# Two graph layers on one Trainium2 core: scores in seven block products instead of eight, and another order of the stages

## The chip, the cores and the metric

The kernel runs on one core of a Trainium2 chip. The metric is the time of one execution on the device, in microseconds (us). Three runs of the kernel before gave 1820.88, 1821.27 and 1821.62 us; the median is 1821.27. One further execution was recorded by the profiler; every duration in this document comes from such a record.

## The reference, cut to what matters

The input x holds 64 items of 256 tokens with 512 features. `adj` is a 256 x 256 matrix of zeros and ones. Two layers follow each other:

```
h   = relu(layernorm(x))
q, k, v = h Wq^T, h Wk^T, h Wv^T
rel = adj^T * (q k^T)                  # elementwise mask, per item 256 x 256
rel = rel / norm(rel, axis=2)
x   = x + rel v
h   = relu(layernorm(x))
x   = x + (adj h) weight + bias
```

Everything is in f32.

## The kernel before, in words

**Tiling.** Two items make a pair of 512 tokens; there are NP = 32 pairs, and the loop in `pairs` (line 431) turns once per pair. Wq and Wk are folded into one matrix M once at the start, so that scores are h M h^T. The stages of a pair are:

- `ln0` (L224): layer norm and ReLU of x into h. `norm` (L186) is statistics on VectorE (L196, L197), a square root on ScalarE (L199) and a few small operations.
- h^T: `place_blocks` (L245) moves the 32 x 32 blocks of h to their transposed places by 16 DMAs on the SP queue, into the tile hp; `transpose_blocks` (L256) then transposes inside each block on VectorE (L260), eight instructions.
- `project_g` (L266), G = M^T h^T, and `project_v` (L279), v = h Wv^T.
- `scores` (L292): h G, 16 matmuls of 256 moving columns; mask on VectorE (L304), squares on ScalarE (L305), a sum of squares on GpSimd (L307).
- `attend` (L310): the product with v (L317, banks pu), the norms (L326, pn: a column of ones times the sums of squares), and x + rel v (L331).
- `norm` again and `ln1_relu` (L337): the ReLU result h2c is split into an fp32r part (cast on ScalarE, L220) and the rest (subtraction on VectorE, L221), together h2s; h2c has two buffers, each for one of the four 128-token chunks. GpSimd adds the bias to x (L346).
- `gather` (L348): adjacency times h2s (L360, banks py), 32 fp32r matmuls, copied to yt by ScalarE (L364).
- `mix` (L372): the last product, with `weight`, added to x (L377); then the transfer out (L381) on the queue of GpSimd.

**The seven block products.** G, V and the last product are done by the scheme of `winograd` (L140), Strassen's algorithm in Winograd's form: each matrix is cut in 2 x 2 blocks, sums of blocks are made first (`left_sums` L127, `right_operands` L111), and seven block products take the place of eight. The products go into three PSUM banks, a, b and c. Banks a and c are not cleared between products: a product adds to what the bank holds, and `take` reads the bank after each. So a product into a bank waits for the reader of the product before in that bank:

```python
        product(bank_a, 6, False)
        take(0, 1, bank_a, True)
        product(bank_c, 3, False)
        take(0, 1, bank_c, False)
        product(bank_a, 7, False)
        take(1, 1, bank_a, False)
        product(bank_b, 2, True)
        take(0, 0, bank_b, False)
        product(bank_a, 4, False)
        take(1, 0, bank_a, True)
```

The first time a block of the result is taken it is copied by ScalarE, the second time it is added by VectorE (in `mix`, always added by VectorE). Scores alone are done by eight block products' worth of plain matmuls.

**What sets the order.** Each engine works through its own instructions in order. A scheduler that runs when the kernel is built puts the instructions of each engine in an order, starting from that of the program and by its own estimates of when each operand is ready; it inserts the waits. PSUM has seven banks for products (`ps_m`), taken in turn, and one for pn. Tiles of the pool `work` have one buffer each: h^T (`ht`), its sums (`hs`), G, v, rel, h2s, yt. The loads of x rotate through four tiles of `xpool`, after a first tile of its own.

In the loop before, turn i puts on TensorE: scores(i), last product(i-1), product with v and pn(i), G(i+1), V(i+1), adjacency(i).

Of the kernel before, what the change touches and what calls it, by code (L numbers as in the profile page):

```python
# [9 lines left out]
F32 = mybir.dt.float32  # L10
# [8 lines left out]
def kernel(  # L19
# [33 lines left out]
    nc = tc.nc  # L53
# [16 lines left out]
    const = ctx.enter_context(tc.tile_pool(name="const", bufs=1))  # L70
    xpool = ctx.enter_context(tc.tile_pool(name="xpool", bufs=4))
    work = ctx.enter_context(tc.tile_pool(name="work", bufs=1))
# [4 lines left out]

    X, H, HP, HT, HS, G, V, R, H2, Y, YS = ({} for _ in range(11))

    def load(i):  # L80
        pool, tag = (const, "x_first") if i == 0 else (xpool, "x")
        X[i] = pool.tile([P, NB, NC, D], F32, tag=tag, name=f"x_{i}")
        nc.sync.dma_start(out=X[i], in_=xs[i])
# [26 lines left out]

    def right_operands(w, name):  # L111

        def blk(j, k):
            return w[:, j * HC : (j + 1) * HC, k * HD : (k + 1) * HD]

        t = [const.tile([P, HC, HD], F32, name=f"{name}_t{n}") for n in range(1, 5)]
        nc.vector.tensor_sub(t[0], blk(0, 1), blk(0, 0))
        nc.vector.tensor_sub(t[1], blk(1, 1), t[0])
        nc.vector.tensor_sub(t[2], blk(1, 1), blk(0, 1))
        nc.vector.tensor_sub(t[3], blk(1, 0), t[1])  # L120
        return {1: blk(0, 0), 2: blk(1, 0), 3: blk(1, 1), 4: t[3], 5: t[0], 6: t[1], 7: t[2]}

# [3 lines left out]

    def left_sums(at, tag, i):  # L127
        s = work.tile([P, 4, HC, HT_], F32, tag=tag, name=f"{tag}_{i}")
        a = left_blocks(at)
        nc.vector.tensor_add(s[:, 0], a(1, 0), a(1, 1))  # L130
        nc.vector.tensor_sub(s[:, 1], s[:, 0], a(0, 0))
        nc.vector.tensor_sub(s[:, 2], a(0, 0), a(1, 0))
        nc.vector.tensor_sub(s[:, 3], a(0, 1), s[:, 1])
        return s

    def left_operands(at, s):
        a = left_blocks(at)
        return {1: a(0, 0), 2: a(0, 1), 3: s[:, 3], 4: a(1, 1), 5: s[:, 0], 6: s[:, 1], 7: s[:, 2]}

# [33 lines left out]
    def product_weights_moving(left, right):  # L173
# [9 lines left out]
        return product  # L183


    def norm(src):  # L186

        st = small.tile([P, TC, 6], F32, tag="st", name="st")
        mv = small.tile([P, TC, 2], F32, tag="mv", name="mv")
        rs = small.tile([P, TC], F32, tag="rs", name="rs")
        nb = small.tile([P, TC], F32, tag="nb", name="nb")
        for c in range(TC):
            nc.vector.bn_stats(st[:, c, :], src[:, c, :])  # L196
            nc.vector.bn_aggr(mv[:, c, :], st[:, c, :])  # L197
        nc.vector.tensor_scalar(rs, mv[:, :, 1], 0.0, EPS, op0=ALU.max, op1=ALU.add)
        nc.scalar.activation(rs, rs, AF.Sqrt)  # L199
        nc.vector.reciprocal(rs, rs)  # L200
        nc.vector.scalar_tensor_tensor(nb, mv[:, :, 0], -1.0, rs, op0=ALU.mult, op1=ALU.mult)  # L201
        return rs, nb

    def relu_chunk(dst, src, scale_shift, c):
        rs, nb = scale_shift
        nc.scalar.activation(  # L206
            dst, src[:, c, :], AF.Relu, bias=nb[:, c : c + 1], scale=rs[:, c : c + 1]
        )
# [13 lines left out]


    def ln0(i):  # L224
        pool, tag = (const, "h_first") if i == 0 else (work, "h")
        H[i] = pool.tile([P, TC, D], F32, tag=tag, name=f"h_{i}")
        relu(H[i], flat(X[i]), norm(flat(X[i])))

    def new_ht(i):
        HT[i] = work.tile([P, DC, NC, NB * P], F32, tag="ht", name=f"ht_{i}")  # L230
        return HT[i]

    def transposes_by_matmul(i):
        h, ht = H.pop(i), new_ht(i)
        for d in range(DC):
            pt = ps_m.tile([P, T], F32, tag="pm", name="pt")
            for half in range(NC):
                for b in range(NB):
                    nc.tensor.transpose(
                        pt[:, ts(half * NB + b, P)], h[:, b * NC + half, ts(d, P)], ident  # L240
                    )
            nc.scalar.copy(ht[:, d].rearrange("p h t -> p (h t)"), pt)
        HS[i] = left_sums(ht, "hs", i)

    def place_blocks(i):  # L245

        h = H.pop(i)
        HP[i] = work.tile([P, TC, DC, P], F32, tag="hp", name=f"hp_{i}")
        hv = h.rearrange("p c (d e) -> p c d e", e=P)
        for j in range(P // S):  # L250
            for k in range(P // S):
                nc.sync.dma_start(
                    out=HP[i][ts(j, S), :, :, ts(k, S)], in_=hv[ts(k, S), :, :, ts(j, S)]
                )

    def transpose_blocks(i):  # L256
        hp, ht = HP.pop(i), new_ht(i)
        for d in range(DC):
            for half in range(NC):
                nc.vector.transpose(  # L260
                    ht[:, d, half].rearrange("p (b n) -> p b n", b=NB),
                    hp.rearrange("p (b h) d n -> p b h d n", b=NB)[:, :, half, d],
                )
        HS[i] = left_sums(ht, "hs", i)

    def project_g(i):  # L266
# [9 lines left out]

        winograd(product_tokens_moving(left_operands(HT[i], HS[i]), m_right), take)

    def project_v(i):  # L279
# [9 lines left out]

        winograd(product_weights_moving(left_operands(HT[i], HS[i]), wv_right), take)  # L290

    def scores(i):  # L292
        ht, g = HT.pop(i), G.pop(i).rearrange("p e h (b n) -> p e h b n", b=NB)
        rel = work.tile([P, NB, NC, N], F32, tag="rel", name=f"rel_{i}")
        sq = work.tile([P, NB, NC, N], F32, tag="sq", name=f"sq_{i}")
        for b in range(NB):
            pm = ps_m.tile([P, NC, N], F32, tag="pm", name="prel")
            for m in range(NC):
                for e in range(DC):
                    nc.tensor.matmul(  # L300
                        pm[:, m, :], ht[:, e, m, ts(b, P)], g[:, e, :, b, :],
                        start=(e == 0), stop=(e == DC - 1),
                    )
            nc.vector.tensor_mul(rel[:, b], pm, adj_sb)  # L304
            nc.scalar.activation(sq[:, b], rel[:, b], AF.Square)  # L305
        sqs = work.tile([P, NB, N], F32, tag="sqs", name=f"sqs_{i}")
        nc.gpsimd.tensor_tensor(sqs, sq[:, :, 0], sq[:, :, 1], ALU.add)  # L307
        R[i] = (rel, sqs)

    def attend(i):  # L310
        (rel, sqs), v, xt = R.pop(i), flat(V.pop(i)), flat(X[i])
        pu = []
        for b in range(NB):
            for n in range(NC):
# [6 lines left out]
                pu.append(pm)  # L321
        pn = ps_n.tile([P, TC], F32, tag="pn", name="pn")
        for b in range(NB):
            for n in range(NC):
                c = b * NC + n
                nc.tensor.matmul(pn[:, c : c + 1], sqs[:, b, ts(n, P)], ones, start=True, stop=True)  # L326
        rn = small.tile([P, TC], F32, tag="rn", name="rn")
        nc.scalar.activation(rn, pn, AF.Sqrt)  # L328
        nc.vector.reciprocal(rn, rn)
        for c in range(TC):  # L330
# [38 lines left out]
    def gather_sums(i):  # L369
        YS[i] = left_sums(Y[i], "ys", i)  # L370

    def mix(i):  # L372
# [5 lines left out]

        winograd(product_weights_moving(left_operands(Y.pop(i), YS.pop(i)), w_right), take)
        if i + 1 < NP:  # L380
# [44 lines left out]
    ln0(0)  # L425
    m_right = right_operands(m_sb, "m")
    wv_right = right_operands(wvt_sb, "wv")
    w_right = right_operands(w_sb, "w")


    def pairs(exact):
        for j in (1, 2):
            if j < NP:
                load(j)
        transposes_by_matmul(0)
        if NP > 1:
            ln0(1)
            place_blocks(1)
        project_v(0)
        project_g(0)  # L440
        for i in range(NP):
            nxt = i + 1 < NP
            if i + 3 < NP:
                load(i + 3)
            scores(i)
            if i > 0:
                gather_sums(i - 1)
            if i > 0 and nxt:
                mix(i - 1)
            if nxt:  # L450
                transpose_blocks(i + 1)
            attend(i)
            if nxt:
                project_g(i + 1)
            scale_shift = norm(flat(X[i]))
            if nxt:
                project_v(i + 1)
            elif i > 0:
                mix(i - 1)
            ln1_relu(i, scale_shift, exact)  # L460
            if i + 2 < NP:
                ln0(i + 2)
                place_blocks(i + 2)
            gather(i, exact)
        gather_sums(NP - 1)
        mix(NP - 1)

# [34 lines left out]
```

## Time and profile before

| | |
|---|---|
| median of 3 runs | 1821.27 us |
| profiled execution: its own time / span of its instructions | 1820.87 / 1819.1 us |
| PE (TensorE matmul) busy | 1790.7 us, 98% |
| DVE (VectorE) busy | 1003.3 us, 55% |
| ACT (ScalarE) busy | 534.4 us, 29% |
| POOL (GpSimd) busy | 254.5 us, 14% |
| granted TensorE clock | 0.999 of full speed |
| HBM traffic | 39 GB/s over the span |

How to read it: the span runs from the first to the last instruction of the program; the 1.8 us between it and the execution's own time lie around it. "PEld" is TensorE's weight load, which overlaps its matmuls. An f32 matmul is recorded as two passes, each with a weight load; a pass starts when the one before has streamed its columns, so the distance between starts, not the duration of one record, is its cost. In a row of instructions the arrow points from what is read to what is written ("out<-in"), then come shapes, count, busy time and mean duration, and after the bar the idle time of that engine just before and what ended it. In a timeline row the first two numbers are start and length in us. Engines that are not the bottleneck may idle without cost.

### The profile page before, as it was taken

How to read it: one execution, taken by the hardware profiler on the slowest of the kernel's cores; microseconds unless marked ns; L12 is line 12 of the kernel's file. 1: busy time of each engine (PE TensorE's matmuls, PEld its weight loads, DVE VectorE, ACT ScalarE, POOL GpSimd, SP SyncE). 2: the span in 40 equal slices, each digit the busy share in tenths (PEclk: the TensorE clock that was granted, in tenths of full speed). 3: DMA queues.
4: the chain of work that ended last, by engine and by line, in shares of the span. 5: the costliest groups of instructions: out<-in, count | busy, mean ns of one | idle time of the engine just before them, and what ended most of it. 6: DMA issues, size and time to landing. Idle time of an engine off the chain costs nothing.

```text
span 1819.1 us, 21280 instructions
## 1 busy us (share of the span) xinstructions
PE 1790.7 (98%) x8262; PEld 1470.8 (81%) x8262; DVE 1003.3 (55%) x1992; ACT 534.4 (29%) x943; POOL 254.5 (14%) x200
## 2 busy tenths in 40 slices
PE   7999999999999999999999999999999999999998
PEld 4788887888888888878888878888788888788886
DVE  4555566545556545665455565456654555654554
ACT  3223332223332133322233321333222333213321
POOL 0101111111111011111011110111110111101111
PEclk9999999999999999999999999999999999999999
DMA  6122221221221222212212212222122122122101
GB/s 223 21 47 47 47 70 49 68 70 24 70 60 57 70 47 47 70 50 68 70 24 70 61 56 70 47 47 70 50 66 70 24 70 62 55 70 47 24 24 49
DMA packets 290239, 105.83 MB, mean 58 GB/s; under 512 B 263120, under 2 KB 263120, under 8 KB 290128
## 3 DMA queue, kind: packets, MB, share of 16 engines
q1 hardware_dynamic: 279904, 68.19, 17.9%
q0 software_dynamic: 8592, 33.03, 4.8%
q10 hardware_dynamic: 1632, 3.15, 0.5%
q8 instruction: 67, 1.10, 0.2%
q14 instruction: 44, 0.36, 0.1%
HBM read 38.27 MB, written 33.55 MB: 39 GB/s over the span
## 4 chain that ended last, share of the span: by engine, by line
PE 66%; DVE 23%; ACT 9%; DMA 1%; issue 1%; DVEq 0%; ACTq 0%
PE bank_a L178 19%; PE prel L300 12%; PE pu L317 12%; DVE st L196 8%; PE py L360 7%; PE bank_c L178 7%; DVE h2s L221 7%; PE bank_b L178 6%; DVE x L331 4%; ACT h2c L206 4%; DVE g L275 2%; ACT h2s L220 2%; ACT v L286 2%; ACT h L206 1%; PE pn L326 1%; PE bank_a L166 1%
## 5 line engine op out<-in xcount | busy, mean ns | idle before, releaser
L346 POOL TENSOR_TENSOR x<-x,bias_bc 128x512 f32<-128x512 f32 x128 | 187.9, 1494 | 526.2 <-ACT h2c L206 512.8
L300 PE MATMUL prel<-g,ht 128*128 128x256 f32 x1024 | 226.4, 379 | 0.7 <-ACT g L273 0.7
L317 PE MATMUL pu<-v,rel 128*128 128x512 f32 x512 | 224.9, 592 | 0.0
L300 PEld LDWEIGHTS prel<-g,ht 128*128 128x128 f32 x1024 | 192.3, 190 | 26.0 <-ACT g L273 1.1
L317 PEld LDWEIGHTS pu<-v,rel 128*128 128x128 f32 x512 | 97.3, 190 | 108.8 <-issue 107.1
L221 DVE TENSOR_TENSOR h2s<-h2c,h2s 128x512 fp32r<-128x512 f32 x128 | 128.4, 1041 | 83.6 <-ACT h2s L220 83.6
L328 ACT ACTIVATE rn<-pn 128x4 f32<-128x4 f32 x32 | 5.5, 173 | 564.1 <-PE pn L326 564.1
L196 DVE BATCH_NORM_STATS2 st<-x 128x6 f32<-128x512 f32 x256 | 167.1, 665 | 7.2 <-DMA x<-in_x_dram 7.2
L377 DVE TENSOR_TENSOR x<-bank_a,x 128x512 f32<-128x512 f32 x128 | 88.4, 691 | 108.1 <-PE bank_a L178 108.1
L307 POOL TENSOR_TENSOR sqs<-sq 128x512 f32<-128x512 f32 x32 | 40.6, 1268 | 699.0 <-issue 594.5
L360 PE MATMUL py<-adjt_r,h2s 128*128 128x256 f32 x1024 | 134.8, 289 | 0.1
L178 PE MATMUL bank_a<-wv_t,hs 128*128 128x256 f32 x512 | 127.0, 391 | 7.4 <-ACT v L286 5.1
L360 PEld LDWEIGHTS py<-adjt_r,h2s 128*128 128x128 f32 x1024 | 127.3, 191 | 2.5 <-DVE h2s L221 0.8
L178 PEld LDWEIGHTS bank_a<-wv_t,hs 128*128 128x128 f32 x512 | 92.5, 190 | 40.9 <-ACT v L286 30.7
L206 ACT ACTIVATE h2c<-x,nb,rs 128x512 f32<-128x512 f32 x128 | 100.7, 810 | 80.8 <-DVE mv L197 53.1
L178 PE MATMUL bank_a<-w_t,ys 128*128 128x256 f32 x512 | 121.1, 379 | 1.2 <-DVE x L377 1.2
L166 PE MATMUL bank_a<-hs,m_t 128*128 128x256 f32 x512 | 121.0, 379 | 0.0
L178 PEld LDWEIGHTS bank_a<-w_t,ys 128*128 128x128 f32 x512 | 97.2, 190 | 14.7 <-DVE x L377 1.6
L166 PEld LDWEIGHTS bank_a<-hs,m_t 128*128 128x128 f32 x512 | 97.3, 190 | 13.2
L304 DVE TENSOR_TENSOR rel<-prel,adj_sb 128x512 f32<-128x512 f32 x64 | 44.2, 691 | 115.3 <-PE prel L300 115.3
L206 ACT ACTIVATE h<-x,nb,rs 128x512 f32<-128x512 f32 x128 | 96.8, 807 | 30.3 <-DVE nb L201 30.3
L305 ACT ACTIVATE sq<-rel 128x512 f32<-128x512 f32 x64 | 40.3, 629 | 206.4 <-DVE rel L304 206.4
(104 smaller groups left out, 2712.4 us busy)
## 6 DMA issues: line engine op xcount, KB each, us to landing
x<-in_x_dram SPq DMA_DIRECT2D x32, 1024.0 KB, 5.5
hp<-h SPq DMA_DIRECT2D x496, 64.0 KB, 2.3
out_dram<-x POOLq DMA_DIRECT2D x31, 1024.0 KB, 4.8
wk_sb<-in_L_gnn_Wk_dram ACTq DMA_DIRECT2D x4, 256.0 KB, 5.5
wq_sb<-in_L_gnn_Wq_dram SPq DMA_DIRECT2D x4, 256.0 KB, 6.5
wv_sb<-in_L_gnn_Wv_dram ACTq DMA_DIRECT2D x1, 1024.0 KB, 11.7
w_sb<-in_L_gnn_weight_dram ACTq DMA_DIRECT2D x1, 1024.0 KB, 15.8
out_dram<-x SPq DMA_DIRECT2D x2, 512.0 KB, 3.4
```

The source lines that it names most:

```text
L166: nc.tensor.matmul(bank[:, e * HT_ : (e + 1) * HT_], right[n][:, d, ts(e, P)], left[n][:, d, :], start=(start and e == 0 and d == 0), stop ...
L178: nc.tensor.matmul(bank[:, b * HD : (b + 1) * HD], left[n][:, d, ts(b, P)], right[n][:, d, :], start=(start and b == 0 and d == 0), stop=( ...
L196: nc.vector.bn_stats(st[:, c, :], src[:, c, :])
L206: nc.scalar.activation(dst, src[:, c, :], AF.Relu, bias=nb[:, c : c + 1], scale=rs[:, c : c + 1])
L221: nc.vector.tensor_sub(dst[:, 1, c, :], h, dst[:, 0, c, :].bitcast(F32))
L300: nc.tensor.matmul(pm[:, m, :], ht[:, e, m, ts(b, P)], g[:, e, :, b, :], start=(e == 0), stop=(e == DC - 1),)
L304: nc.vector.tensor_mul(rel[:, b], pm, adj_sb)
L317: nc.tensor.matmul(pm[:, :D], rel[:, b, m, ts(n, P)], v[:, b * NC + m, :], start=(m == 0), stop=(m == NC - 1),)
L331: nc.vector.scalar_tensor_tensor(xt[:, c, :], pu[c][:, :D], rn[:, c : c + 1], xt[:, c, :], op0=ALU.mult, op1=ALU.add,)
L346: nc.gpsimd.tensor_tensor(xt[:, c, :], xt[:, c, :], bias_bc, ALU.add)
L360: nc.tensor.matmul(pm[:, d, :], left[:, b * NC + m, ts(d0 + d, P)], right, start=(n == 0), stop=(n == len(terms) - 1),)
L377: nc.vector.tensor_add(dst, bank.rearrange("p (b e) -> p b e", b=NB), dst)
```

## The change

It has four parts.

1. **Scores by seven block products.** `scores` calls `winograd` with a new product of 128-column matmuls (28 per pair, `product_of_tokens`). The right operands are sums of blocks of G, made on VectorE by the new `score_sums`. Blocks are taken from PSUM into rel by ScalarE copies and VectorE additions (L339 after), and the mask is then applied to rel in SBUF (L343), in place of the mask on the way out of PSUM.
2. **A new order of stages.** Turn i now calls: product with v(i), V(i+1), layer norm(i), scores(i+1), transposes(i+2), adjacency(i), G(i+2), ReLU and block DMAs(i+3), sums of G(i+2), last product(i). pn now comes ahead of the product with v. Two instructions of `ln0` are held in program order. Ahead of the loop stand V(0), G(0), sums and scores(0), G(1) and its sums.
3. **Buffers.** h^T and its sums get two buffers (pool `twice`). x goes round a ring of four tiles in all, and the transposed-block tile becomes one constant tile, `blocks`, in which h of pair 0 is kept at first.
4. **Sums in place.** One of the four sums of the left operands, and of the right ones, is written over a block that is not needed any more, so that three extra tiles suffice in place of four. The number of operations stays at four.

```diff
+    def right_operands(b, t):
+        nc.vector.tensor_sub(t[1], b(1, 1), b(0, 1))
+        nc.vector.tensor_sub(b(0, 1), b(0, 1), b(0, 0))
+        nc.vector.tensor_sub(t[0], b(1, 1), b(0, 1))
+        nc.vector.tensor_sub(t[2], b(1, 0), t[0])
+        return {1: b(0, 0), 2: b(1, 0), 3: b(1, 1), 4: t[2], 5: b(0, 1), 6: t[0], 7: t[1]}
...
+    def product_of_tokens(left, right):
+        def product(bank, n, start):
+            for b in range(NB):
+                for d in range(HC):
+                    nc.tensor.matmul(
+                        bank[:, ts(b, P)], left[n][:, d, ts(b, P)], right[n][:, d, ts(b, P)],
...
+    def score_sums(i):
+        g = G.pop(i)
+        t = work.tile([P, 3, HC, HT_], F32, tag="gt", name=f"gt_{i}")
+        G[i] = right_operands(
+            lambda j, k: g[:, j * HC : (j + 1) * HC, k], [t[:, n] for n in range(3)]
+        )
...
     def scores(i):
...
-            nc.vector.tensor_mul(rel[:, b], pm, adj_sb)
-            nc.scalar.activation(sq[:, b], rel[:, b], AF.Square)
+        def take(t, k, bank, first):
+            dst = rel[:, :, t, ts(k, P)]
+            src = bank[:, :HT_].rearrange("p (b n) -> p b n", b=NB)
+            if first:
+                nc.scalar.copy(dst, src)
+            else:
+                nc.vector.tensor_add(dst, src, dst)
+        winograd(product_of_tokens(left, right), take)
+        for t in range(NC):
+            nc.vector.tensor_mul(
+                rel[:, :, t], rel[:, :, t], adj_sb[:, t : t + 1, :].to_broadcast([P, NB, N])
+            )
+            nc.scalar.activation(sq[:, :, t], rel[:, :, t], AF.Square)
...
+        project_v(0)
+        project_g(0)
+        score_sums(0)
+        scores(0)
+        if NP > 1:
+            transpose_blocks(1)
+            project_g(1)
+            score_sums(1)
...
         for i in range(NP):
+            if 0 < i < NP - 3:
+                load(i + 3)
+            if not last:
+                attend(i)
+                project_v(i + 1)
+                ln1_relu(i, norm(flat(X[i])), exact)
+                scores(i + 1)
+            if i + 2 < NP:
+                transpose_blocks(i + 2)
+            gather(i, exact)
+            gather_sums(i)
+            if i + 3 < NP:
+                scale_shift = ln0_norm(i + 3)
+            if i + 2 < NP:
+                project_g(i + 2)
+            if i + 3 < NP:
+                ln0_relu(i + 3, scale_shift)
+                place_blocks(i + 3)
+            if i + 2 < NP:
+                score_sums(i + 2)
...
+            mix(i)
```

The seven products of `winograd` are unchanged, and so are the matmuls of G, V, the product with v, the adjacency and the last product.

## The prediction

> **What bounds the kernel now.** I read the page's busy shares first, then one turn of the loop (one pair of batch items) by stage, then who held TensorE up, then the timeline. The loop repeats every 55.55 us: the first product with v of one pair starts at 1175.22 us, that of the next at 1230.77.
>
> ```profile
> PE 1790.7 (98%) x8262; PEld 1470.8 (81%) x8262; DVE 1003.3 (55%) x1992; ACT 534.4 (29%) x943; POOL 254.5 (14%) x200
> ...
> L300 PE MATMUL prel<-g,ht 128*128 128x256 f32 x1024 | 226.4, 379 | 0.7 <-ACT g L273 0.7
> ```
>
> TensorE is busy 98% of the span and VectorE 55%: on average TensorE is the bound. The second line is the scores product that the change replaces: 1024 records are 32 pairs x 32 passes (an f32 matmul is recorded as two passes).
>
> ```profile
> 1152.56:1156.40 3.84, 3.84 (x33) 3.84 (x33) 0.32 (x1) 2.35 (x4) 0.00 (x0) 1.00 0.64 99
> 1156.40:1163.30 6.90, 6.90 (x33) 6.07 (x33) 3.15 (x5) 1.22 (x2) 0.00 (x0) 1.00 0.47 70
> 1163.30:1175.40 12.10, 12.10 (x57) 10.66 (x57) 5.52 (x9) 0.63 (x1) 1.26 (x1) 1.00 0.00 0
> 1175.40:1183.10 7.70, 7.70 (x25) 3.88 (x25) 5.23 (x11) 0.03 (x1) 0.77 (x1) 1.00 0.39 145
> 1183.10:1195.20 12.10, 12.10 (x57) 10.65 (x57) 10.64 (x29) 4.25 (x9) 1.24 (x2) 1.00 0.23 83
> 1195.20:1208.11 12.91, 12.65 (x59) 10.51 (x58) 6.26 (x9) 7.92 (x14) 4.65 (x4) 1.00 0.12 16
> ```
>
> The columns are stage, its length, then busy time of PE, weight loads, DVE, ACT, POOL. The stages are adjacency (32 passes), scores (32), last product (56), product with v and its norms pn (16 + 8), G (56), V (56). All but one are exactly passes times pace: 6.90/32 = 0.216 us for a pass of 256 columns, 3.84/32 = 0.120 for an fp32r pass of the adjacency product, 6.87/16 = 0.429 for 512 columns. Only V takes 12.91 instead of 12.10. The cause is one wait, twice per turn:
>
> ```profile
> PEld bank_a L178 <- ACT v L286: 1.1, 2, 0.6
> ```
>
> So a turn is 54.8 us of passes and 0.75 us of stall. VectorE is the point to watch: over a turn it has 31.1 us of work, but beside G it was busy 10.64 of 12.10 us. That stage holds the work that follows the product with v; its rows are these:
>
> ```profile
> 1183.56 2.73 DVE L331 SCALAR_TENSOR_TENSOR x<-pu,rn,x 128x512 f32<-128x512 f32 x4
> ...
> 1193.06 1.52 ACT L206 ACTIVATE h2c<-x,nb,rs 128x512 f32<-128x512 f32 x2 [1.90 <-DVE mv L197]
> ...
> 1194.49 1.12 ACT L220 CAST h2s<-h2c 128x512 fp32r<-128x512 f32 x2
> ...
> 1195.12 2.38 DVE L221 TENSOR_TENSOR h2s<-h2c,h2s 128x512 fp32r<-128x512 f32 x2 [0.89 <-ACT h2s L220]
> ...
> 1199.36 1.64 DVE L221 TENSOR_TENSOR h2s<-h2c,h2s 128x512 fp32r<-128x512 f32 x2 [1.87 <-ACT h2s L220]
> ...
> 1207.76 4.18 PE L360 MATMUL py<-adjt_r,h2s 128*128 128x256 f32 x32
> ```
>
> The split h2s was done at 1201.0 and its product started at 1207.76: the two projections between (25 us) covered the chain with 7 us to spare. The change spends this cover.
>
> **What the Trainium skill says.** "TensorE: Matmul & The Clock Gate", LDWEIGHTS, puts a weight load at columns/1.2 GHz, 107 ns for 128 columns; the trace agrees (loads of pn follow each other at 0.112 us, transposes of 128 columns at 0.109). "SBUF — State Buffer" says VectorE operations with two SBUF inputs and GpSimd operations take a shared port pair as an exclusive lock; the trace agrees as far as it goes: L221 has a minimum of 675 ns, a median of 900 and a maximum of 1775, and the long ones lie beside the bias adds on POOL. "VectorE: DVE Perf Modes", the errata section, prices an fp32 two-tensor operation at (N+151)/0.96 ns: 691 for 512 elements (the trace has 691) and, as an estimate, 424 for the 256-element additions of the new scores, which the trace does not show.
>
> **The change, part by part.** Times t below count from the start of the product with v in one turn.
>
> *Scores on TensorE.* Removed: 32 passes at 0.216 = 6.91 us. Added: 7 products x 4 matmuls x 2 = 56 passes of 128 columns. No f32 product of that width is in the trace; its floor is 107 ns of load. From below 0.109 (transposes, 128 columns), from above 0.120 (adjacency, which also pairs a load of 128 columns with about as long a stream); a loss cannot be excluded, since loads last 190 ns where they have time, and at that pace the stage would be 10.6 us. I take 0.112: 6.27 us, 0.64 saved per turn (0.8 to 0.2).
>
> *Scores on the other engines.* DVE: four 512-element sums of G (L120 to L123, 0.69 each, +2.8 us), three additions of 0.42 (+1.3), masks unchanged. ACT: four copies of 256 elements, some 0.4 each. DVE goes from 31.1 to 35.2 us a turn. The sums of G run beside G's end and the last product, scores come 20 us later: nothing on the path. In-place sums (left operands, weights) have the count of before: nothing.
>
> *The new order.* TensorE now runs pn, product with v of pair i, V(i+1), scores(i+1), adjacency(i), G(i+2), last product(i). Between the product with v and the adjacency product lie 12.1 + 6.3 us instead of 25. VectorE's order, which the build fixes, puts behind the residual adds and layer norm of pair i, in one row: the h2s subtractions with V's three additions between them, eight transposes of pair i+2, its four sums, two statistics of pair i+3, and between these last the additions of the scores. The last of the seven scores products reuses bank a and needs VectorE's addition of the product before last (L339). TensorE waits there in order, and behind it stand 29 of the 32 adjacency passes, G and all else. So this chain decides:
>
> - Product with v ends at 6.87. Fourth residual add: 0.27 until VectorE sees it (mix: 1164.86 to 1165.13), 0.74; statistics 0.70, aggregate 0.20; scale, square root (behind V's first copy on ACT, 0.46), reciprocal, shift: 1.2. First h2c at 10.0.
> - First to second part of the split: two h2c and two casts took 2.06 us in the rows above (1193.06 to 1195.12); now a V copy of 0.46 stands between. First subtraction at 12.6; two take 2.38: 15.0.
> - The fourth h2c waits for the second subtraction (two buffers): 0.71 + cast 0.61 + 0.15 latency: 16.45. Two subtractions as before, 0.95 and 0.69, with a V addition of 0.65 between: 18.7.
> - Eight transposes at 0.345 and one V addition: 22.1.
> - Four sums (0.57 to 0.65 each as they are spaced), two statistics 0.61 each, one aggregate, two additions: 4.55. Addition done at 26.65, TensorE released at 26.7.
>
> TensorE by itself would be there at 6.87 + 12.10 + 48 x 0.112 + 3 x 0.12 = 24.7. It stalls 2.0 us per turn, about 0.8 of it already in V (fourth product, bank a, after V's second addition at 18.0 against 17.2). The rest: last scores product 0.9 + 0.1 for restarting, 29 adjacency passes 3.5, G 12.1, last product 12.1, pn 0.9: 56.3. One more wait is near: G's third copy stands behind two ReLUs of pair i+3 on ACT, and comes about when bank a is needed again; 0.1. **Turn: 56.4 us**, against 55.55.
>
> *Waits that go.* V's stall on ACT (0.75) is absorbed in that sum. pn ahead of the product with v frees the residual adds from waiting for all four banks: part of the chain above. pn needs sqs, done 20 us earlier: nothing.
>
> *Moved transfers.* On SP stand the load of x and 16 block transfers. Load of i+3: last product ends at -0.9, out transfer issued and landed by 5.5 (1176.67 to 1181.53), load landed at 11.5; first used at 22. Blocks of i+3 start with the last ReLU at 45, 10.9 us of issue and 2.3 to land: 58, which is 2 of the next turn, used at 18.7. Cover 10 and 16 us, no cost; without it each would stop VectorE in the chain above. POOL's order is unchanged.
>
> *Head and tail.* The sums of pair 0 now stand between G(0) and its scores, and pn(0) right behind these scores, waiting for masks, squares and POOL: 57.3 (G ends), 59.5, 64.9, sqs at 68.6, pn, G(1): first product with v at 81.6. Then 30 turns, then product with v, V, scores, adjacency, pn: 30.9, and the end as before from the last product with v on (45.6 less pn's 0.9): 157.3 in all.
>
> **Sum.** 157.3 + 30 x 56.4 = 1849.3 us of span; the profiled run lies 1.8 above its span (1820.87 against 1819.1), so 1851 us. That run is 0.4 below the median of the runs, 1821.27, within what I resolve. Break-even is a turn of 55.4, that is a chain shorter by 1.0 us.
>
> **Rivals.** (1) TensorE at its own pace, and so faster: VectorE reaches the addition L339 before 25.7. Then a turn is 54.2 to 55.2, the middle giving 157.3 + 30 x 54.7 + 1.8 = 1800. For it: VectorE has 20 us of slack a turn, and it idles from about 9 to 12.6 while ACT works, so a different overlap can gain a us. Against: the row of 20 us above has only waits in it that I could price from rows. (2) Weight-bound scores: at 0.190 per pass the last product is free at 29.5, a turn is 59.7, and about 1957 comes out. Against: 0.109 to 0.120 in three other rows. (3) The change does what it says but gain and stall cancel: turn at 55.4, 1821. The product does change: the new program holds 28 matmuls of 128 columns per pair.
>
> **Chances and range.** VectorE's chain, slower: 0.70, with 1825 to 1880 as its own range (a chain 0.9 shorter or longer by one us per turn). Rival 1: 0.20. Rival 2: 0.04. Rival 3: 0.06. Faster or slower by over 0.2% (3.6 us, about what a measurement of this kernel can tell from no change): 0.20 and 0.74. Leaving out half of rival 1, rival 2 and the chain's upper end: 1800 to 1885.
>
> **What would show it.** The turn in the timeline; the distance of passes in the new scores (0.112); TensorE's wait for L339 and for V's addition L317, 2 us together; L213 without a wait for a load and L289 without one for blocks. Wrong it is if TensorE shows no wait of over 0.3 us for VectorE, or if scores take over 8 us without a wait.

## The result, and the profile after

On the same chip the kernel before gave a median of 1821.32 us (4 runs), the changed kernel 1827.95 us (4 runs, 1826.08 to 1829.72): a ratio of 1.0036, with a 95% interval of 1.0019 to 1.0054. The change is slower by about 6.6 us; 1851 was forecast. The profiled execution took 1829.72 us, the longest of the four; its span is 1827.5 us, 8.4 more than before.

Busy shares, from the page of the kernel after:

```profile
PE 1774.1 (97%) x9030; PEld 1479.1 (81%) x9030; DVE 1150.8 (63%) x2216; ACT 571.8 (31%) x1071; POOL 243.9 (13%) x200
```

The scores products, from its groups of instructions:

```profile
L195 PE MATMUL bank_a<-gt,hs 128*128 128x128 f32 x512 | 67.6, 275 | 0.0
...
L195 PE MATMUL bank_a<-gt,ht 128*128 128x128 f32 x256 | 36.8, 287 | 25.7 <-DVE rel L339 25.7
```

TensorE has 16.6 us less work than before, and yet the span grew. Of the seven scores products, six start without delay in the loop (0.0 after the second bar in the first line, which holds two of them). The last one, which reuses bank a, has waited 25.7 us in all for VectorE's addition L339. This line of one group already names the wait.

The stages of one turn (the columns as in the table of before; here V, scores with three adjacency passes in it, the other 29 adjacency passes, G):

```profile
540.91:553.19 12.28, 12.28 (x57) 10.47 (x56) 8.11 (x16) 6.74 (x12) 5.48 (x4) 1.00 0.24 84
553.19:560.89 7.70, 6.80 (x61) 6.59 (x59) 7.70 (x20) 1.71 (x4) 0.00 (x0) 1.00 0.01 2
560.89:564.44 3.55, 3.55 (x32) 3.55 (x31) 1.53 (x5) 3.04 (x6) 1.08 (x1) 1.00 0.00 0
564.44:576.55 12.11, 12.11 (x58) 10.56 (x57) 6.21 (x12) 4.56 (x8) 0.22 (x1) 1.00 0.01 2
```

In the second row VectorE is busy for all of the 7.70 us, and TensorE for 6.80 of them: for this one stage VectorE is the bound, although it is busy 63% over the span. A turn is 55.49 us, against 55.55 before. The waits of TensorE's weight loads say the same (total, times, longest), and the second line is what stays of V's wait:

```profile
PEld bank_a L195 <- DVE rel L339: 31.7, 29, 1.1
...
PEld bank_a L183 <- DVE v L317: 10.6, 31, 1.5
```

The row on VectorE that the prediction worked out, in the turn whose product with v starts at 533.96:

```profile
546.51 2.01 DVE L240 TENSOR_TENSOR h2s<-h2c,h2s 128x512 fp32r<-128x512 f32 x2 [2.57 <-ACT h2s L239]
...
550.01 0.69 DVE L240 TENSOR_TENSOR h2s<-h2c,h2s 128x512 fp32r<-128x512 f32 x1 [0.89 <-ACT h2s L239]
...
552.31 0.76 DVE L289 STREAM_TRANSPOSE ht<-blocks 128x256 f32<-128x256 f32 x2
...
555.55 0.64 DVE L139 TENSOR_TENSOR hs<-ht 128x512 f32<-128x512 f32 x1
...
559.50 0.41 DVE L339 TENSOR_TENSOR rel<-bank_a,rel 128x256 f32<-128x256 f32 x1
...
559.97 1.16 PE L195 MATMUL bank_a<-gt,ht 128*128 128x128 f32 x8 [0.90 <-DVE rel L339]
```

From 552.31 on VectorE never pauses until the addition at 559.50 is done at 559.91, and TensorE starts its last scores product 0.06 us later. The product whose result that addition takes had ended at 557.8. This addition, of bank a, is the second of the three of L339 in a turn (bank c at 558.57, bank a at 559.50, bank b at 559.84); the expectations below call it the third.

**Where the time went.** The products with v of the first and of the last pair, before and then after:

```profile
65.12 7.03 PE L317 MATMUL pu<-v,rel 128*128 128x512 f32 x16
...
1773.51 7.03 PE L317 MATMUL pu<-v,rel 128*128 128x512 f32 x16
...
89.86 7.03 PE L366 MATMUL pu<-v,rel 128*128 128x512 f32 x16
...
1784.54 7.11 PE L366 MATMUL pu<-v,rel 128*128 128x512 f32 x16
```

The first one starts at 89.86 us instead of 65.12: +24.7. The thirty turns give back 1.1 (1664.5 us instead of 1665.6), the way to the last pair's product with v 12.7 (30.15 instead of 42.80), the end from there 2.6 (42.96 instead of 45.59). The sum is 24.7 - 1.1 - 12.7 - 2.6 = 8.3, against 8.4 between the spans. About 12.1 us of the longer start and of the shorter end are one product G, which the new order does one pair earlier. So what makes the change slower is its start: start and end together take 9.4 us more. The loop, which should have gained 0.64 us for the passes and 0.75 us for V's stall in each turn, gained 0.04.

### The profile page after: what moved, and what is told of

The parts are those of the page before. It is cut to its first block, busy times and chain, and to the rows that moved or that the text cites. A ratio compares the mean times of both kernels' runs of the same rounds, so it can differ in the third digit from the quotient of the medians.

```text
span 1827.5 us, 23023 instructions
## 1 busy us (share of the span) xinstructions
PE 1774.1 (97%) x9030; PEld 1479.1 (81%) x9030; DVE 1150.8 (63%) x2216; ACT 571.8 (31%) x1071; POOL 243.9 (13%) x200
## 4 chain that ended last, share of the span: by engine, by line
PE 67%; DVE 18%; ACT 9%; issue 5%; DMA 0%; DVEq 0%; POOL 0%; POOLq 0%
PE bank_a L183 15%; PE pu L366 12%; PE bank_a L171 12%; PE py L401 6%; PE bank_c L183 6%; PE bank_c L171 6%; DVE h2s L240 5%; ACT h2c L225 5%; DVE ht L289 4%; PE bank_b L183 3%; PE bank_b L171 3%; PE bank_a L195 2%; ACT v L315 2%; ACT h2s L239 2%; PE pn L357 1%
## 5 line engine op out<-in xcount | busy, mean ns | idle before, releaser
L387 POOL TENSOR_TENSOR x_ring<-x_ring,bias_bc 128x512 f32<-128x512 f32 x128 | 176.5, 1397 | 372.9 <-ACT h2c L225 372.9
L240 DVE TENSOR_TENSOR h2s<-h2c,h2s 128x512 fp32r<-128x512 f32 x128 | 124.7, 993 | 107.3 <-ACT h2s L239 107.3
L213 DVE BATCH_NORM_STATS2 st<-x_ring 128x6 f32<-128x512 f32 x256 | 174.0, 681 | 10.9 <-DMA x_ring<-in_x_dram 6.7
L315 ACT COPY v<-bank_a 128x512 f32<-128x512 f32 x96 | 55.9, 583 | 356.5 <-PE bank_a L183 356.5
L418 DVE TENSOR_TENSOR x_ring<-bank_a,x_ring 128x512 f32<-128x512 f32 x128 | 88.2, 689 | 85.2 <-PE bank_a L183 85.2
L422 POOL DMA_DIRECT2D out_dram<-x_ring x31 | 23.9, 770 | 768.8 <-issue 336.3
L372 DVE SCALAR_TENSOR_TENSOR x_ring<-pu,rn,x_ring 128x512 f32<-128x512 f32 x128 | 96.0, 750 | 45.9 <-PE pu L366 43.9
L183 PE MATMUL bank_a<-wv_t,hs 128*128 128x256 f32 x512 | 121.0, 379 | 0.0
L302 ACT COPY g<-bank_a 128x512 f32<-128x512 f32 x96 | 55.5, 579 | 199.4 <-PE bank_a L171 199.4
L225 ACT ACTIVATE h2c<-x_ring,nb,rs 128x512 f32<-128x512 f32 x128 | 97.4, 806 | 29.6 <-DVE h2s L240 15.6
L225 ACT ACTIVATE h<-x_ring,nb,rs 128x512 f32<-128x512 f32 x124 | 97.1, 809 | 14.8 <-DVE nb L220 14.7
```

What stands on the lines that cost most here:

```text
L183: nc.tensor.matmul(bank[:, b * HD : (b + 1) * HD], left[n][:, d, ts(b, P)], right[n][:, d, :], start=(start and b == 0 and d == 0), stop=( ...
L213: stats = nc.vector.bn_stats(st[:, c, :], src[:, c, :])
L225: return nc.scalar.activation(dst, src[:, c, :], AF.Relu, bias=nb[:, c : c + 1], scale=rs[:, c : c + 1])
L240: nc.vector.tensor_sub(dst[:, 1, c, :], h, dst[:, 0, c, :].bitcast(F32))
L315: nc.scalar.copy(dst, src)
L372: nc.vector.scalar_tensor_tensor(xt[:, c, :], pu[c][:, :D], rn[:, c : c + 1], xt[:, c, :], op0=ALU.mult, op1=ALU.add,)
```

## The experiments

The theory: **(A)** TensorE's wait in the scores is set by VectorE's row up to the addition of bank a (L339); what stands in that row ahead of the addition is paid for in every turn. Without it TensorE needs 54.3 to 54.4 us a turn. The rivals are in each expectation. All ratios are to the kernel before on the same chip, with 95% intervals; "turn" is the distance between the first products with v of successive pairs, which repeats within 0.02 us in nearly every turn. In the diffs `behind(a, b)` stands for an added order: a comes after b on its engine, with no data between them.

### Statistics out of the row

The statistics of pair i+3 come behind the last of the sums of yt.

```diff
-            if in_order and c == 0:
-                tc.keep_in_program_order(stats)
+            if in_order is not None:
+                behind(stats, in_order)
...
+        return norm(flat(X[i]), in_order=last_sum["ys", i - 3])
```

> Theory A (VectorE's row of work is what the last scores product waits for): the row ahead of the addition L339 loses two statistics and an aggregate, 1.3 us; the wait of 1.1 us per turn falls under 0.2, a turn takes 54.3 to 54.6 us in place of 55.49, and the whole 1793 to 1803 us. Rival B (the wait only changes its place, for the sums of yt and the statistics of pair i+3 now come later and hold G or the last product): a wait of about 1 us turns up in G or in the last product, the turn stays at 55.3 to 55.6 and the whole at 1822 to 1830 us.

1811.32 us, ratio 0.9945 (0.9932 to 0.9959); turn 54.95. What is left of the wait:

```profile
PEld bank_a L204 <- DVE rel L348: 16.8, 30, 0.6
```

The wait is halved and not gone: with the statistics away, the addition of bank a ends 25.08 us after the start of the product with v (t = 25.08) instead of 25.95, but three adjacency passes (0.36 us) that filled part of the wait now stand behind the last product. 55.49 - 0.87 + 0.36 = 54.98, against 54.95 measured. The direction is A's, the size about half of what was expected.

### The start

```diff
+                if i == 0 and c == 0 and 1 in last_g:
+                    behind(mm, last_g[1])
...
+        if i == 0 and NP > 1:
+            behind(recip, last_sum["hs", 1])
```

Here pn(0) goes behind G(1) on TensorE, and the reciprocal behind the sums of h^T of pair 1 on VectorE.

> The start alone is changed: the norms of pair 0 (pn and the reciprocal behind it) come behind G and the left sums of pair 1. Theory A (the start lost time because TensorE and VectorE waited in order for these norms and the clock fell after the pause): first product with v at 84 to 86 us in place of 89.9, turns as in the changed kernel, whole 1822 to 1825 us. Rival B (the start is late since the blocks of pair 1 land late): G of pair 1 starts no earlier than 74 us and the whole stays at 1826 to 1830 us.

1824.24 us, ratio 1.0016 (1.0009 to 1.0023). The first product with v starts at 84.73 instead of 89.86, and the turns stay at 55.49. So pn(0), put ahead of G(1), costs the start 5.1 us by these two traces and 3.7 us by the medians, and has nothing to do with the loop. The trace of the changed kernel had a slow start: with the same start, that of the run "One sum more" below reaches the first product with v at 87.79.

### The new order alone

Scores by 16 plain matmuls as before, without sums of G and with four tiles again for the sums of h^T; everything else of the change kept:

```diff
+        for b in range(NB):
+            pm = ps_m.tile([P, NC, N], F32, tag="pm", name="prel")
+            for m in range(NC):
+                for e in range(DC):
+                    nc.tensor.matmul(
+                        pm[:, m, :], ht[:, e, m, ts(b, P)], g[:, e, :, b, :],
+                        start=(e == 0), stop=(e == DC - 1),
+                    )
+            nc.vector.tensor_mul(rel[:, b], pm, adj_sb)
-        winograd(product_of_tokens(left, right), take)
```

> The new order with the scores of before (16 matmuls of 256 columns, mask on the way out of PSUM, left sums not in place). Theory A (the order alone takes away V's wait for ACT, 0.75 us, and the seven block products bring their own wait): a turn of 54.9 to 55.2 us with no wait of TensorE over 0.3 us, whole 1810 to 1818 us, faster than both. Rival B (the order itself costs, through the shorter cover between the product with v and the adjacency product): a wait of about 1 us ahead of the adjacency product or of G, a turn of 55.5 or more, whole 1823 us or more.

1814.86 us, ratio 0.9965 (0.9951 to 0.9979); turn 55.03, and no wait of TensorE over 0.3 us in a turn. The order, with its buffers, gains about 6 us by itself: 0.52 us in each of the thirty turns, where V's wait on ScalarE goes, less what the start loses (first product with v at 88.59). Plain scores never wait for VectorE inside the stage, as no bank is used twice in it. Block scores on top, although they hold 0.64 us less work a turn, cost 13 us.

### The block scores alone, in the old order

```diff
                 project_g(i + 1)
+                score_sums(i + 1)
...
+        winograd(product_of_tokens(left, right), take)
```

> The old order with scores by seven block products. Theory A (in the old order VectorE has little to do beside scores): passes of 0.112 us give 0.64 us per turn, a wait for the addition of scores of at most 0.3, V's wait of 0.75 stays; a turn of 55.0 to 55.3 us, whole 1806 to 1815 us. Rival B (the wait for the addition belongs to block products in any order, since a product of 0.9 us leaves its reader too little time): a wait of 1 us and more per turn inside scores, a turn of 55.7 or more, whole 1827 us or more.

1894.2 us, ratio 1.0403 (1.0389 to 1.0418); from the second turn on 57.3 a turn, but 58.7 to 59.0 in 13 of the 29, mostly every other one. Neither theory had the place right: the scores take 6.25 us there without any wait, and it is V that waits.

```profile
PEld bank_a L178 <- ACT v L299: 102.2, 59, 3.0
```

The timeline beside V shows why:

```profile
546.27 2.38 DVE L234 TENSOR_TENSOR h2s<-h2c,h2s 128x512 fp32r<-128x512 f32 x2 [0.83 <-ACT h2s L233]
548.57 1.75 DVE L312 TENSOR_TENSOR gt<-g 128x512 f32<-128x512 f32 x1
550.36 1.65 DVE L313 TENSOR_TENSOR g<-g 128x512 f32<-128x512 f32 x1
552.04 0.69 DVE L314 TENSOR_TENSOR gt<-g 128x512 f32<-128x512 f32 x1
...
554.98 0.81 ACT L219 ACTIVATE h<-x,nb,rs 128x512 f32<-128x512 f32 x1 [3.39 <-DVE nb L214]
```

The sums of G came to stand between the two h2s pairs, where GpSimd adds the bias: two of them take 1.75 and 1.65 us instead of 0.69. ScalarE waits for the shift `nb` that stands behind them (last row), and its copies of V stand behind that. TensorE's pause in V, 2.57 to 2.59 us, is the same in all 29 turns; in the 13 longer ones the granted clock fell to 0.50 behind it (last section).

### The old order with these sums later

```diff
-                score_sums(i + 1)
...
+            if nxt:
+                score_sums(i + 1)
             gather(i, exact)
```

The first sum of G is also put behind the last addition of V.

> The old order with the scores by seven block products, the four sums of G now behind the last addition of V on VectorE instead of between the h2s operations. Theory A (the 2.6 us wait in V of the run in the old order came from these sums alone): that wait goes, turn 54.7 to 55.3 us, 1795 to 1815 us, so that the old order carries the block scores as well as the new one does. Rival B (the wait in V is ScalarE's, which is too full there): a wait of 1 us or more stays in V, turn 56 us or more, 1838 us or more.

1801.43 us, ratio 0.9892 (0.9877 to 0.9907); turn 54.83. Theory A of this run: the sums' place was all of it. The block scores alone, in the old order and with one buffer for h^T, gain 19 us. V keeps a wait of 0.5 us a turn on ScalarE there.

### Two sums of h^T out of the row

Here `last_take` is the last of the three additions of L339.

```diff
+        if tag == "hs" and i - 1 in last_take:
+            behind(third, last_take[i - 1])
```

> The changed kernel with the third and fourth sums of h^T of pair i+2 held behind the three additions of the scores of pair i+1 on VectorE; nothing else changes in what is computed. Theory A (VectorE's row between the transposes and the additions ends the turn): two sums of 0.68 us leave the row ahead of the third addition, one of them with a pause behind it, the three adjacency passes that filled 0.6 us of TensorE's wait go back behind the last product; the wait of 1.1 us falls to 0.3 to 0.6 us, a turn goes from 55.49 to 54.9 to 55.1 us, 1809 to 1816 us. Rival B (the additions are not the cause, something else holds the last product back): turn 55.4 to 55.5, 1825 to 1829 us.

1820.88 us, ratio 1.0004 (0.9996 to 1.0012); turn 55.30. The gain is smaller than A expected. The gap that the two sums left was filled when the kernel was built: a third statistic (0.6 us) moved ahead of the additions. The addition of bank a ends 0.54 us earlier than in the changed kernel and the 0.36 us of adjacency passes go behind the last product: 55.49 - 0.54 + 0.36 = 55.31, against 55.30 measured. The end of the addition still sets the turn; what I had wrong is that an order given for one instruction moves others.

### All three moves

Statistics, sums of h^T and start together, the three diffs above.

> The changed kernel with all three moves on VectorE and in the start: statistics of pair i+3 behind the sums of yt, third and fourth sums of h^T behind the additions of the scores, and in the start pn of pair 0 behind G of pair 1 and its reciprocal behind the sums of h^T of pair 1. Theory A (the only wait in a turn is that of the last scores product on VectorE): no wait of TensorE over 0.3 us in a turn, turn 54.3 to 54.5 us, first product of v at 84 to 85 us, whole 1786 to 1796 us. Rival B (TensorE's own pace with these stages is not under 54.9, another engine comes next): turn 54.9 or more, 1805 us or more.

1787.9 us, ratio 0.9822 (0.9809 to 0.9836): faster than both kernels, and the best version here. Turn 54.31, first product with v at 83.64. Now VectorE waits for TensorE, not the reverse:

```profile
542.03 0.42 DVE L351 TENSOR_TENSOR rel<-bank_a,rel 128x256 f32<-128x256 f32 x1 [0.40 <-PE bank_a L206]
...
542.73 1.06 PE L206 MATMUL bank_a<-gt,ht 128*128 128x128 f32 x8
```

The last product has no idle time in brackets. This is TensorE's own pace, as rival 1 of the prediction had it.

### One sum more

```diff
         nc.vector.tensor_sub(s[:, 2], a(0, 1), s[:, 1])
+        if tag == "hs" and i > 1:
+            nc.vector.tensor_sub(s[:, 2], a(0, 1), s[:, 1])
```

> The changed kernel with the last sum of h^T, from pair 2 on, done twice on VectorE (same result): one instruction of 0.68 us more in the row. Theory A (VectorE's row sets the turn, without slack): it lies ahead of the third addition, turn 55.49 plus 0.6 to 0.8 us, 1845 to 1852 us. Rival B (VectorE has slack there, TensorE's own stages or weight loads set the turn): 1826 to 1830 us.

1828.4 us, ratio 1.0039 (1.0025 to 1.0053); turn 55.51: no change. Taken by the numbers this is rival B. But the experiment missed its aim, as the rows show:

```profile
558.26 0.42 DVE L341 TENSOR_TENSOR rel<-bank_a,rel 128x256 f32<-128x256 f32 x1
...
558.92 0.69 DVE L144 TENSOR_TENSOR hs<-ht,hs 128x512 f32<-128x512 f32 x1
```

The added sum (L144) was put behind the addition, which ends at the same t as in the changed kernel. So it tells only that 0.69 us behind the addition costs nothing. A run with the added work ahead of it was needed.

### A longer row, ahead of the addition

On top of all three moves, where nothing else can fill or leave the row:

```diff
-        nc.vector.tensor_sub(s[:, 0], a(0, 0), a(1, 0))
+        for _ in range(4 if tag == "hs" and i > 1 else 1):
+            nc.vector.tensor_sub(s[:, 0], a(0, 0), a(1, 0))
```

> The run with all three moves, with the first sum of h^T done four times from pair 2 on (same result): three instructions of 0.68 us more on VectorE ahead of the third addition, of which one addition moves ahead of the second sum. Theory A (the third addition on VectorE's row sets the turn once the slack is used up): it starts 1.3 us later than now, 0.2 us of that is slack, turn 54.31 plus 0.9 to 1.3 us, 55.2 to 55.6 us, 1815 to 1828 us. Rival B (TensorE's own pace sets the turn, VectorE has some us of slack): turn 54.3 to 54.5, 1788 to 1794 us.

1825.18 us, ratio 1.0023 (1.0014 to 1.0033); turn 55.55, within the range of A. The wait is back, at the same instruction:

```profile
437.97 2.82 DVE L149 TENSOR_TENSOR hs<-ht 128x512 f32<-128x512 f32 x4
...
441.64 0.42 DVE L352 TENSOR_TENSOR rel<-bank_a,rel 128x256 f32<-128x256 f32 x1
...
442.11 1.16 PE L207 MATMUL bank_a<-gt,ht 128*128 128x128 f32 x8 [0.99 <-DVE rel L352]
```

The addition starts 25.26 us after the product with v instead of 23.89, 1.37 us later, and a turn is 1.24 us longer: all but 0.13 us of what was put ahead of this addition is paid, while behind it 0.69 us were free (the run before).

### No bias on GpSimd

This kernel leaves the bias out.

```diff
-        for c in range(TC):
-            nc.gpsimd.tensor_tensor(xt[:, c, :], xt[:, c, :], bias_bc, ALU.add)
```

> The changed kernel without the addition of the bias on GpSimd (the output lacks the bias). Theory A (beside GpSimd's additions VectorE's h2s operations take 1.0 us where they could take 0.65, and this lies in the row that sets the turn): h2s pairs 1.3 instead of 1.5 to 2.0 us, row 0.5 to 0.9 us shorter, wait 1.1 down to 0.2 to 0.6, turn 54.6 to 55.0, 1803 to 1813 us. Rival B (h2s pairs end with ScalarE's second copy, not with VectorE's operation): pairs keep their end, turn 55.3 to 55.5, 1821 to 1828 us.

1794.92 us, ratio 0.9858 (0.9843 to 0.9873); turn 54.43, faster than expected. The h2s subtractions, in the groups of the changed kernel and of this run:

```profile
L240 DVE TENSOR_TENSOR h2s<-h2c,h2s 128x512 fp32r<-128x512 f32 x128 | 124.7, 993 | 107.3 <-ACT h2s L239 107.3
...
L240 DVE TENSOR_TENSOR h2s<-h2c,h2s 128x512 fp32r<-128x512 f32 x128 | 85.5, 688 | 100.0 <-ACT h2s L239 100.0
```

Their mean is 688 ns, against 993 ns in the changed kernel (124.7 us for 128). The addition of bank a ends 24.90 us after the start of the product with v instead of 25.95, and of TensorE's wait 0.03 us is left. "SBUF — State Buffer" of the Trainium skill, the part on the shared port pair, has an exclusive lock between VectorE's operations with two SBUF inputs and GpSimd's that read SBUF; this run agrees, and prices GpSimd's additions in this row at 1.05 us a turn.

### One buffer each for h^T and its sums

```diff
-        return twice.tile([P, DC, NC, NB * P], F32, tag="ht", name=f"ht_{i}")
+        return work.tile([P, DC, NC, NB * P], F32, tag="ht", name=f"ht_{i}")
...
-        HL[i] = left_operands(twice, ht, "hs", i)
+        HL[i] = left_operands(work, ht, "hs", i)
```

> The changed kernel with one buffer each for h^T and for its sums, as before the change. The transposes of pair i+2 then have to wait until the last scores product of pair i+1 has read h^T, and stand behind the third addition on VectorE. Theory A (it is the place of transposes and sums ahead of the additions that costs the 1.1 us, and the second buffer is what lets them stand there): no wait for the additions of the scores; transposes and sums end later, the second or third product of G waits 0.3 to 1 us for them; turn 54.6 to 55.4 us, 1802 to 1824 us. Rival B (the second buffer is needed, G comes too early for the transposes): a wait of 2 us or more in G, turn 56.5 us or more, 1855 us or more.

1798.0 us, ratio 0.9872 (0.9857 to 0.9887); turn 54.43, better than A expected:

```profile
549.40 0.42 DVE L339 TENSOR_TENSOR rel<-bank_a,rel 128x256 f32<-128x256 f32 x1 [0.40 <-PE bank_a L195]
...
552.29 2.39 DVE L289 STREAM_TRANSPOSE ht<-blocks 128x256 f32<-128x256 f32 x7
...
556.61 1.96 PE L171 MATMUL bank_c<-ht,m_sb 128*128 128x256 f32 x8
```

With one buffer the transposes have to stay behind the last scores product, and so behind the additions. G's first product starts at 554.82, its second at 556.61, 1.79 us later, where 1.73 is its own pace: the late transposes cost G 0.1 us (12.22 us instead of 12.11). **The second buffers, of h^T and of its sums, cost the changed kernel 30 us.** They do not slow the row (the first pair of h2s subtractions takes 2.0 us in both kernels); they allow an order in which transposes, sums and statistics, some six us of work that is not urgent, stand ahead of an addition that TensorE waits for. (What is shown is the effect of the order that goes with one buffer: the transposes moved with it.)

### The start of V

With all three moves, the sums of the weights moved behind those that V(0) needs:

```diff
+        rights["wv"] = weight_operands(wvt_sb, wv_t)
         transposes_by_matmul(0)
+        rights["m"] = weight_operands(m_sb, m_t)
+        rights["w"] = weight_operands(w_sb, w_t)
```

> The run with all three moves, and in the start the sums of the weights moved behind those that the first products need: wv's sums and M's in turns, then those of h^T of pair 0, w's last. Theory A (the second product of V of pair 0 waits 2.6 us for the in-place sum of h^T, which is queued behind the weights' sums, and runs at half pace after it): first product of v 1 to 4 us earlier than 83.6, whole 1784 to 1787 us. Rival B (the sums of wv end later instead): no gain, 1787 to 1791 us.

1788.15 us, ratio 0.9818 (0.9805 to 0.9832), the same as without; first product with v at 84.24. V's second product waits 3.65 us for the in-place sum instead of 2.57 in the run with all three moves, but starts at 35.76 instead of 36.67. Behind the longer pause this trace has the clock granted at 0.55 over 3.46 us, where the other has 1.00; that takes the 0.9 us back. Rival B: no gain from this order.

## Why the prediction was wrong in size, step by step

It had the instruction right and what it waits for, and the size of the wait wrong: 30 us of increase against 6.6. On the spans the differences are: start +8.3 us (81.6 forecast, 89.86 found), thirty turns -27.5 (1692 against 1664.5), end -2.6; in sum 1849.3 - 21.8 = 1827.5.

That the sign came out is in good part luck. The forecast had the loop slower by 25.5 us (thirty times 56.4 against 55.55) and start and end longer by 3.8. Found are a loop 1.1 us shorter, and start and end 9.4 us longer. With the start and end of the forecast, 157.3, the measured turns give 157.3 + 1664.5 + 1.8 = 1823.6 us, hardly more than before. In the loop gain and stall cancel, which is what rival 3 said: it had a turn of 55.4.

- **Scores on TensorE**: right. The passes follow each other at 0.112 us (1668 distances read 0.111 or 0.112), and the stage without its wait is 6.27 us. The weight-bound rival (0.190) is out.
- **The chain on VectorE (the step that failed)**: the links were right, their sum was 0.7 us too long. The prediction calls the addition that of the product before last; it takes the fifth of the seven products, the last one into bank a before, and the chain was summed for it. Times t after the start of the product with v:

| link | forecast | measured |
|---|---|---|
| first subtraction | 12.6 | 12.55 |
| two subtractions done | 15.0 | 14.56 |
| third subtraction | 16.45 | 16.05 |
| transposes begin | 18.7 | 18.35 |
| transposes and V addition done | 22.1 | 21.6 |
| addition of bank a done | 26.65 | 25.95 |
| TensorE released | 26.7 | 26.0 |

The largest term is the pair of subtractions: 2.38 us was carried over from a row of before, and took 2.01 here. Before, the second of the two was the long one (1.76 us), here the first (1.41), so they meet GpSimd's additions at another point; without these the pair takes 1.29. Transposes with V's addition lost 0.15, and the section of sums, taken as 4.55, took 4.36. The other 0.2 us of a turn are the two tenths that I added for a restart and for G: next to nothing of either is there (559.97 to 560.89 for the last product, 12.11 for G).
- **V's share of the stall**, forecast as 0.8: V takes 12.28, 0.18 over its passes. The addition that its last product waits for ended at t = 17.34 instead of 18.0, since the row ran early. With this TensorE comes to the last scores product at 24.87, where I had 24.7.
- **The stall**: forecast 2.0 in all, measured 1.1 in scores and 0.18 in V. A turn of 56.4 was forecast and is 55.49. The prediction gave a break-even turn of 55.4; with the start and end as found it is 55.2, and the 0.28 us by which the mean turn of 55.48 is longer make, thirty times, the 8.4 us of the spans. This is the term to learn from. The sum of a 26 us chain with an error of 3% decides over a wait of 1 us, and the error is multiplied by thirty. Of the 0.9 us a turn, the pair of subtractions is 0.37, transposes 0.15, the sums 0.19, restart and G 0.2.
- **Waits that go, transfers that move**: right. No load and no block transfer stops VectorE in a turn, and V's stall on ScalarE is gone, as the run with plain scores (55.03 a turn) shows by itself.
- **The start**: "in-place sums: nothing" did not hold there. V's second product waits for one; before (first row) the same sum was done 1.45 us sooner. In the changed kernel V(0) then runs at half speed:

```profile
34.74 1.97 PE L178 MATMUL bank_c<-wv_t,hs 128*128 128x256 f32 x8 [1.40 <-DVE hs L130]
...
36.19 3.65 PE L183 MATMUL bank_c<-wvt_sb,ht 128*128 128x256 f32 x8 [2.58 <-DVE ht L140]
```

The same stretch, and the first products of G(1), by window:

```profile
36.19:39.65 3.46, 3.46 (x9) 2.71 (x10) 3.46 (x8) 0.00 (x0) 0.00 (x0) 0.51 0.02 5
...
74.65:81.50 6.85, 6.85 (x18) 5.22 (x19) 4.78 (x11) 2.71 (x5) 0.00 (x0) 0.56 0.36 49
```

The column after POOL's is the granted clock, 0.51 and 0.56. By the trace, pn(0) starts 3.0 us late, nearly all of it from V(0), G(1) starts 2.2 us later after pn than I had it, and takes 15.2 us instead of 12.1. The run with pn(0) behind G(1) took 5.1 of these 8.3 us away.

Of the 3.0 us, 1.7 are the half clock, and they vary from one execution to the next: of the nine traces with this pause of 2.58 us the clock fell in three and stayed at 1.00 in six, and from V's second product to the second of scores it took 26.6 us in this trace and 24.9 in those six. Around the pause ahead of pn(0), 2.8 to 3.2 us long, the clock fell in all seven traces that have one, for 3.4 to 10.2 us. The in-place sums of M come in another order and start at 29.11 us instead of 27.87; that this makes the sum of V(0) late is read from the traces, and no run took it back.
- **Rival 1** (TensorE at its own pace, 54.7 a turn, 1800 us) is what comes out once the row is out of the way by any of three means: 54.31 with all moves, 54.43 without the bias, 54.43 with one buffer. It had the pace within its range of 54.2 to 55.2, and was wrong that VectorE would be in time.

So the wait needs at least two parts of the change together: block scores, which use bank a again and so need VectorE inside the stage; and the second buffers, which let the transposes stand ahead. Plain scores (55.03) and one buffer (54.43) each take it away. A third is likely and not shown: the new order, which leaves 18 us between the product with v and the end of the scores. The old order with one buffer has no such wait (54.83), but the old order with two was not tried. Nor was it tried how much of the first ten us of the row, norm, ReLU and cast, could be shortened.

## What to carry to other kernels

When an engine empties a bank that TensorE uses again within a stage, list what the built order puts ahead of that instruction on its engine: only that counts, and a mean utilisation of 63% says nothing on it. A second buffer is also a licence for the scheduler to start unurgent work early, so after adding one look at what the early work now stands ahead of. Where a forecast is a small difference of long chains, take each link's duration as a span from its shortest to its longest row, and put the break-even next to it.

## What the runs showed of the hardware

- The length of a pause of TensorE does not by itself decide whether its granted clock falls. With block scores in the old order V pauses 2.57 to 2.59 us in each of 29 turns. In 13 of them the clock was then 0.50 for 3.41 us, and the turn 1.4 to 1.7 us longer; in 16 it stayed at 1.00. One product of each kind:

```profile
265.07 3.61 PE L178 MATMUL bank_a<-wv_t,hs 128*128 128x256 f32 x8 [2.57 <-ACT v L299]
...
324.03 1.99 PE L178 MATMUL bank_a<-wv_t,hs 128*128 128x256 f32 x8 [2.58 <-ACT v L299]
```

- In the start of the changed kernel the clock was 0.51 for 3.46 us after a pause of 2.58 us (passes at 0.427 us instead of 0.216); pauses of 0.9 us in every turn left it at 1.00. "TensorE: Matmul & The Clock Gate", Part 1, of the Trainium skill puts the time at half clock at about 3.4 us, and the idle time that leads to it at no less. The traces agree with the first for these stretches (behind pn(0), with more pauses in it, one lasted 10.24 us) and differ on the second: 2.57 us of idle time was enough here.
- A two-input VectorE operation of 512 f32 elements took 1.65 to 1.75 us beside GpSimd's additions and 0.69 without: more than twice (block scores in the old order).
- The scores matmuls of 128 columns show records of 275 ns that start every 112 ns. Taking the mean duration of a group for its cost would have put the stage at 15 us.
